# A fused attention and FP4 network block on one core: projection lead, network lag and the place of a rounding changed

## The chip, the core and the metric

The kernel runs on one core of one Trainium2 chip. The metric is device time in microseconds (us) of one execution, as the median of several runs; lower is better. The core has five engines that work side by side, each through its own written list of instructions: TensorE (PE, matrix products, with PEld for its weight loads), VectorE (DVE), ScalarE (ACT), GpSimd (POOL) and SyncE (SP), which here issues every DMA.

## What is computed

`x` is 8 sequences of 1024 tokens with 512 features, all float32. Cut to what matters:

```python
xn  = layernorm(x)
qkv = xn @ W_attn + b_attn                      # 512 -> 3 x 512, 16 heads of 32
att = softmax(causal(q @ k.T * 32 ** -0.5)) @ v
attn = att @ W_proj + b_proj
# network: weights [1408, 512], [1408, 512], [512, 1408]; fq = blockwise FP4 round trip
g, u = fq(xn) @ fq(w_gate).T, fq(xn) @ fq(w_up).T
net  = fq(silu(g) * u) @ fq(w_down).T
out  = x + attn + net
```

`fq` scales each block of 16 values by its largest magnitude over 6, rounds to the FP4 grid and scales back. It is applied to the weights, to `xn` and to the hidden values.

## The kernel before

The work comes in 64 tiles of 128 tokens (8 per sequence) and 64 units of attention: a unit is two heads of one sequence, so a sequence has 8 units. Loops run over tiles, units and weight pieces; each is a Python generator that issues some instructions and then says how long it thinks they take.

- `prepare` and `project` take two tiles at a time: normalise (L398 to L405), transpose on PE (L351, copied out by ACT at L352), multiply with the attention weights (L466 for q and k, L511 for v). ACT takes q and k from PSUM with bias and scale (L478, into `full`, two buffers) and v (L522, `full` too). The inner function `split` writes the part of `full` that the float32r format holds to `high` (L491) and what is left to `low`, in place of `full` (L492). Both go to DRAM (L497), and v too (L527). The first AHEAD tiles multiply with attention weights that are kept on chip; the others stream theirs through a ring of DMA loads (L235).
- `weights_quantised` takes the network's weights in 34 pieces of 128 rows and up to 512 columns: DMA load (L367), ten DVE instructions of the FP4 round trip (L320 to L344), transposes on PE (L351), a copy by ACT (L352).
- `maxima` of a unit: scores for the row maxima and sums on PE (L597, float32r, with high and low parts stacked), the maxima on DVE (L610, L622), an exp with a running sum on ACT (L568), then small statistics, one transpose (L655), a round trip through DRAM (L663 to L676) that puts the shifts where PE needs them.
- `weigh` of a unit: transposed scores with the shift added by a second product (L724, L727), exp on ACT (L735), the causal triangle on POOL (L741), the product with v on PE (L706), a copy by ACT (L769).
- `network` of a tile: gate and up products (L831), silu on ACT (L843), product on DVE (L848), the FP4 round trip on DVE, transposes on PE (L351, L352), down product (L809).
- `finish` of a tile: fetch the attention output, add and scale (L927, L928), output product (L936), add (L941), store.

All engines' lists are written by a planner that runs when the kernel is built. It keeps a clock of its own and, for ACT, DVE and POOL, the time when each is expected to be free (`act`, `dve`, `pool`, called with guessed durations). `Later` puts an action on a list of due times. A `Stream` is a row of parts, each with a position at which it begins and a length, counted in units; `merge` picks, of the streams that lie least far along and whose inputs are thought ready, the next to issue. PE's six PSUM banks are handed out by `Banks`; PE, ACT, DVE and SP then run the lists in order, each instruction waiting for its data and its buffer.

The order of the whole: first a phase with the first eight tiles' projections beside weight pieces; then q, k and v of the first units are loaded (L540, L552); then a second phase up to AHEAD tiles, with more weight pieces and the maxima of unit 0; then the main merge. There, with positions counted in units: unit n is weighed at n; maxima of unit n at n - 1.3; the network of tile n at n + LAG, preceded by what is left of the weight pieces, spread over the first LAG units; the FP4 input of tile n at n + LAG - 1; the projection of tile pair n at n - AHEAD; the output of tile n at n + LAST. EARLY is the number of weight pieces spread over the two phases before.

Of the kernel before, what the change touches and what calls it, by code (L numbers as in the profile page):

```python
# [27 lines left out]
def kernel(  # L28
# [31 lines left out]
    nc = tc.nc  # L60
# [6 lines left out]
    NT = S // P  # L67
# [5 lines left out]
    assert NU == NT  # L73
    QG = 4
    W = QG * P
    AHEAD = 2 * NT
    LAG = 2
    LAST = NT + 2
    SOONER = 0.3
    QUEUE = 2.0  # L80
# [76 lines left out]
    def dve(us, after=0.0):  # L157
        return on("dve", us, after)
# [294 lines left out]
    def project(batch, xnT, g, after, first):  # L453
        yield 0.0, after, 1
        for s in range(2):
            for f in range(0, NC, 2):
                if first:
                    halves = [w[:, :, :] for w in resident_a[s * NC + f : s * NC + f + 2]]
                else:
                    wa = ring_a.take()  # L460
                    halves = [wa[:, :, j * P : (j + 1) * P] for j in range(2)]
                k, bank = banks.take()
                pq = bank.rearrange("p (j t) -> p j t", j=2)
                for j in range(2):
                    for c in range(NC):
                        nc.tensor.matmul(  # L466
                            pq[:, j, :],
                            lhsT=halves[j][:, c, :],
                            rhs=xnT[:, c, :],
                            start=(c == 0),  # L470
                            stop=(c == NC - 1),
                        )
                if not first:
                    ring_a.load_in(3.44 + HOP)
                settle(stored)
                full = p2.tile([P, 2, QW], F32, name="full")
                for j in range(2):
                    nc.scalar.activation(  # L478
                        full[:, j, :],
                        pq[:, j, :],  # L480
                        AF.Identity,
                        bias=bqk[:, s, f + j : f + j + 1],
                        scale=SCALE if s == 0 else 1.0,
                    )
                    end = act(QW, clock[0] + 1.7 * (j + 1))
                banks.back(k, end)
                high = p2.tile([P, 2, QW], F32R, name="high")
                low = full.bitcast(F32R)

                def split(full=full, high=high, low=low):  # L490
                    nc.vector.tensor_copy(high, full)  # L491
                    nc.vector.tensor_tensor(low, full, high.bitcast(F32), ALU.subtract)  # L492
                    dve(1.15)

                def store(s=s, f=f, high=high, low=low):
                    for piece, part in ((0, high), (1, low)):
                        nc.sync.dma_start(  # L497
                            out=batch.qk[s, piece, f : f + 2, :, g * QW : (g + 1) * QW].rearrange("f p t -> p f t"),
                            in_=part.bitcast(F32),
                        )  # L500

                stored.append(Later(end - clock[0] - 0.3, split))
                stored.append(Later(end - clock[0] + 2.0, store))
                yield 3.44, 0.0, 1
        for f in range(0, NC, 2):
            wa = resident_a[2 * NC + f // 2] if first else ring_a.take()
            k, bank = banks.take()
            pv = bank.rearrange("p (i t) -> p i t", i=QT)
            for i in range(QT):
                for c in range(NC):  # L510
                    nc.tensor.matmul(  # L511
                        pv[:, i, :],
                        lhsT=xnT[:, c, i * P : (i + 1) * P],
                        rhs=wa[:, c, :],
                        start=(c == 0),
                        stop=(c == NC - 1),
                    )
            if not first:
                ring_a.load_in(3.44 + HOP)
            settle(stored)  # L520
            v_out = p2.tile([P, QT, 2 * P], F32, name="full")
            nc.scalar.copy(v_out, pv)  # L522
            end = act(W, clock[0] + 3.44)
            banks.back(k, end)

            def store(f=f, v_out=v_out):
                nc.sync.dma_start(  # L527
                    out=batch.v[g * QT : (g + 1) * QT, :, f * P : (f + 2) * P].rearrange("t p e -> p t e"), in_=v_out
                )

            stored.append(Later(end - clock[0] + 0.5, store))
            yield 3.44, 0.0, 1
# [516 lines left out]

    N = B * NT  # L1050
    PIECES = sum((w.shape[0] // P) * -(-w.shape[1] // CW) for w in (w_gate, w_up, w_down))
    EARLY = PIECES - 6
    tiles = [Tile(n) for n in range(N)]
    units = [Unit(n) for n in range(N)]
    batches = []
# [2 lines left out]
    with tc.manual_schedule(  # L1058
        engines={
            mybir.EngineType.PE,  # L1060
            mybir.EngineType.Activation,
            mybir.EngineType.DVE,
            mybir.EngineType.Pool,
            mybir.EngineType.SP,
        }
    ):
        for tl in tiles[:QT]:
            load_tokens(tl)
        for k in range(2 * NC):
            w = p8.tile([P, NC, P], F32, name="pr")  # L1070
            nc.sync.dma_start(out=w, in_=wa_in[:, :, k * P : (k + 1) * P])
            resident_a.append(w)
        nc.sync.dma_start(out=bqk, in_=b_attn[0 : 2 * D].rearrange("(s c p) -> p s c", p=P, c=NC))
        nc.vector.tensor_scalar_mul(bqk[:, 0, :], bqk[:, 0, :], SCALE)
        passed(3.0)
        for tl in tiles[:QT]:
            normed(tl)

        weights_steps = weights_quantised()
        for col in range(2 * D, 3 * D, 2 * P):  # L1080
            w = p2.tile([P, NC, 2 * P], F32, name="wa")
            nc.sync.dma_start(out=w, in_=wa_in[:, :, col : col + 2 * P])
            resident_a.append(w)
        part, late = EARLY * 0.25, [0.0]

        def prepared(first, last):
            return itertools.chain(*(prepare(n) for n in range(first, last, QT)))

        merge(
            [  # L1090
                Stream([(prepared(0, NT), 10.8 * NT, 0.0, 1.0)]),
                Stream([(up_to(weights_steps, part, late), part, 0.0, 1.0)]),
            ]
        )
        settle(stored)
        ring_p.load()
        for n, h in ((0, 0), (0, 1), (1, 0), (1, 1)):
            load_half(units[n], h)
        load_values(units[0])
        net = network(tiles)  # L1100
        TILE = sum(4 * 1.72 * w / CW + w / P * 0.97 for _, w in chunks)

        def first_maxima():
            yield 0.0, clock[0] + 6.0, 1
            yield from maxima(units[0])

        merge(
            [
                Stream([(prepared(NT, AHEAD), 10.8 * NT, 0.0, 1.0)]),
                Stream([(up_to(weights_steps, part, late), part, 0.0, 1.0)]),  # L1110
                Stream([(first_maxima(), 6.0, 0.3, 0.7)]),
            ]
        )
        ring_a.load()
        ring_a.load()
        load_biases()

        def last_weights():
            for half in range(2):
                wp = p2.tile([P, NC, 2 * P], F32, name="wa")  # L1120
                nc.sync.dma_start(out=wp, in_=wp_in[:, :, half * 2 * P : (half + 1) * 2 * P])
                resident.append(wp)
            yield 0.0, 0.0, 0

        def networks():
            yield weights_steps, (PIECES - EARLY) * 0.5, 0.0, LAG
            for n in range(N):
                yield up_to(net, TILE), TILE, n + LAG, 1.0

        def preparations():  # L1130
            for n in range(AHEAD, N, QT):
                yield prepared(n, n + QT), 10.8 * QT, n - AHEAD, QT
            yield last_weights(), 1.0, N - AHEAD + 1, 0.0

        merge(
            [
                Stream((weigh(un), 17.5, un.n, 1.0) for un in units),
                Stream((maxima(un), 6.0, un.n - 1 - SOONER, 1.0) for un in units[1:]),
                Stream(networks()),
                Stream((quantised(tl), 0.45, tl.n + LAG - 1, 0.5) for tl in tiles),  # L1140
                Stream(preparations()),
                Stream((finish(tl), 4.5, tl.n + LAST, 1.0) for tl in tiles),
            ]
        )
        passed(100.0)
# [37 lines left out]
```

## Time and profile before

| what | value |
|---|---|
| median of 3 runs (lowest, highest) | 4255.48 us (4254.81, 4258.41) |
| profiled execution, its own time | 4251.42 us |
| its span | 4249.7 us |
| mean granted PE clock | 0.991 |
| instructions | 58555 |
| HBM read, written | 400.56 MB, 169.35 MB |
| chain that ended last: PE, ACT, DVE | 82%, 7%, 4% |
| first L597, first L724, first L831 | 174.9, 290.8, 363.8 us |
| last L724 | 4121.8 us |

The span runs from the first to the last instruction of the profiled execution; its own time has 1.7 us more around it. An engine's busy time is the time in which at least one of its instructions was running; matmul records overlap, so the mean duration of a record is longer than the pace at which records follow each other. A float32 matmul of the program leaves two records, a float32r one (L597, L724, L727) one. From 860.9 us (unit 10) to 3160.9 (unit 46) the trace repeats itself every two units, 127.8 us each time.

### The profile page before, as it was taken

The page shows a single profiled execution, that of the slowest core. Times are in us where ns is not written, and L with a number is a line of the kernel's source. Part 1 is how long each engine was busy: PE and PEld are TensorE (multiplying, and loading weights), DVE is VectorE, ACT ScalarE, POOL GpSimd, SP SyncE. Part 2 cuts the span into 40 slices and gives each one's busy share as a digit, 9 for nine tenths or more (in the row PEclk, how much of TensorE's full clock was granted, in tenths as well). Part 3 has the DMA queues.
Part 4 walks back from the last instruction along what each step waited for, and adds up shares of the span by engine and source line. Part 5 has one row for each costly group of instructions (what it writes and reads, how often), then busy time and mean ns, then how long its engine had stood idle before and what let it go on. Part 6 is the DMA issues. An engine that isn't in the chain of part 4 may idle for free.

```text
span 4249.7 us, 58555 instructions
## 1 busy us (share of the span) xinstructions
PE 4131.2 (97%) x17684; PEld 2619.1 (62%) x17684; DVE 2763.2 (65%) x7323; ACT 2321.8 (55%) x5918; POOL 546.5 (13%) x1296
## 2 busy tenths in 40 slices
PE   7789999999999999999999999999999999999998
PEld 6666666666666666666666666666666555555555
DVE  6786765666575666575666575666565666667755
ACT  2246556565555565555565555565555666666640
POOL 0001111111111111111111111111111111111110
PEclk9889999999999999999999999999999999999999
DMA  5654434455455455455455455455454433333314
GB/s 183 177 173 129 124 103 120 118 157 157 132 155 150 140 164 153 132 156 151 140 160 155 134 154 149 141 162 153 138 149 131 117 92 94 95 92 93 93 56 126
DMA packets 564187, 573.84 MB, mean 135 GB/s; under 512 B 114976, under 2 KB 420128, under 8 KB 563872
## 3 DMA queue, kind: packets, MB, share of 16 engines
q1 hardware_dynamic: 563872, 570.10, 48.3%
q8 instruction: 142, 2.33, 0.2%
q14 instruction: 173, 1.42, 0.1%
HBM read 400.56 MB, written 169.35 MB: 134 GB/s over the span
## 4 chain that ended last, share of the span: by engine, by line
PE 82%; ACT 7%; DVE 4%; DMA 1%; issue 1%; SPq 0%; ACTq 0%; POOL 0%; DVEq 0%
PE bank L831 26%; PE acc L809 12%; PE bank L466 8%; PE y L706 7%; PE bank L724 6%; PE bank L727 6%; PE bank L597 5%; PE bank L936 5%; PE bank L511 4%; ACT bank L568 3%; PE bank L351 2%; ACT L568 1%; ACT L843 1%; ACT pr L735 1%; DMA ks<-y_kept 1%
## 5 line engine op out<-in xcount | busy, mean ns | idle before, releaser
L568 ACT ACTIVATE bank<-bank,neg 128x512 f32<-128x512 f32 (+3 forms) x1536 | 856.7, 559 | 163.7 <-DVE neg L610 119.8
L735 ACT ACTIVATE pr<-bank 128x512 f32<-128x512 f32 (+3 forms) x1536 | 662.7, 494 | 482.6 <-PE bank L727 478.2
L741 POOL TENSOR_SCALAR_AFFINE_SELECT pr<-pr 128x128 f32<-128x128 f32 x1024 | 393.2, 397 | 3238.3 <-ACT pr L735 3228.9
L610 DVE CUSTOM_DVE_ANT_0 bank<-bank,mask 128x128 f32<-128x128 f32 (+3 forms) x1024 | 501.2, 500 | 469.5 <-PE bank L597 455.7
L724 PE MATMUL bank<-shT,pick 128*128 128x512 f32 (+3 forms) x1536 | 683.8, 453 | 2.7 <-DVE hid L848 1.5
L831 PE MATMUL bank<-wuT,xqT 128*128 128x512 f32 (+1 forms) x1536 | 676.1, 565 | 3.9 <-ACT bank L568 1.0
L809 PE MATMUL acc<-wdT,hqT 128*128 128x512 f32 x1408 | 665.4, 596 | 1.3 <-ACT hqT L352 1.3
L831 PE MATMUL bank<-wgT,xqT 128*128 128x512 f32 (+1 forms) x1536 | 662.9, 561 | 0.0
L597 PE MATMUL bank<-ks,qs 128*128 128x512 f32 (+3 forms) x1536 | 636.2, 475 | 24.7 <-ACT bank L568 21.7
L727 PE MATMUL bank<-qs,ks 128*128 128x512 f32 (+3 forms) x1536 | 516.9, 346 | 0.0
L622 DVE TENSOR_REDUCE neg<-bank 128x1 f32<-128x512 f32 x512 | 345.7, 685 | 186.8 <-PE bank L597 185.6
L597 PEld LDWEIGHTS bank<-ks,qs 128*128 128x128 f32 x1536 | 277.5, 191 | 234.1 <-issue 111.3
L831 PEld LDWEIGHTS bank<-wuT,xqT 128*128 128x128 f32 x1536 | 277.0, 190 | 228.8 <-issue 158.9
L831 PEld LDWEIGHTS bank<-wgT,xqT 128*128 128x128 f32 x1536 | 280.0, 190 | 219.3 <-issue 151.9
L724 PEld LDWEIGHTS bank<-shT,pick 128*128 128x128 f32 x1536 | 290.4, 189 | 155.7 <-issue 78.9
L809 PEld LDWEIGHTS acc<-wdT,hqT 128*128 128x128 f32 x1408 | 255.3, 190 | 197.0 <-issue 183.6
L478 ACT ACTIVATE full<-bank,bqk 128x256 f32<-128x256 f32 x256 | 107.4, 470 | 491.1 <-PE bank L466 409.3
L727 PEld LDWEIGHTS bank<-qs,ks 128*128 128x128 f32 x1536 | 290.6, 189 | 110.6 <-issue 77.1
L466 PE MATMUL bank<-xnT,wa 128*128 128x256 f32 x1536 | 349.8, 381 | 0.9 <-ACT xnT L352 0.6
L466 PEld LDWEIGHTS bank<-xnT,wa 128*128 128x128 f32 x1536 | 288.4, 190 | 55.6 <-issue 18.9
L706 PE MATMUL y<-pr,vs 128*32 128x512 f32 (+3 forms) x3072 | 316.5, 501 | 0.8 <-POOL pr L741 0.8
L568 ACT ACTIVATION_READ_ACCUMULATOR bank<-bank,neg 128x1 f32 x1536 | 315.4, 205 | 0.0
(99 smaller groups left out, 4674.7 us busy)
## 6 DMA issues: line engine op xcount, KB each, us to landing
wa<-in_L_attn_W_attn_dram SPq DMA_DIRECT2D x146, 512.0 KB
qs<-qk_kept SPq DMA_DIRECT2D x512, 128.0 KB
ks<-qk_kept SPq DMA_DIRECT2D x512, 128.0 KB
wp<-in_L_attn_W_proj_dram SPq DMA_DIRECT2D x81, 512.0 KB
qk_kept<-high SPq DMA_DIRECT2D x128, 256.0 KB
qk_kept<-full SPq DMA_DIRECT2D x128, 256.0 KB
y_kept<-yu SPq DMA_DIRECT2D x256, 128.0 KB
yT<-y_kept SPq DMA_DIRECT2D x112, 256.0 KB
```

Source lines behind the costliest of these rows:

```text
L466: nc.tensor.matmul(pq[:, j, :], lhsT=halves[j][:, c, :], rhs=xnT[:, c, :], start=(c == 0), stop=(c == NC - 1),)
L568: nc.scalar.activation(part, part, AF.Exp, bias=neg[:, kind, k + j : k + j + 1], scale=1.0 if kind == 1 else -1.0, accum_out=sums[:, kind, ...
L597: nc.tensor.matmul(sc[:, j * n : (j + 1) * n], lhsT=un.qs[Q][:, r, i * P : (i + 1) * P], rhs=un.ks[h][:, r, :n], start=True, stop=True,)
L610: nc.vector.tensor_tensor_reduce(part, part, mask[:, W - n :], scale=-1.0, scalar=3e38, op0=ALU.add, op1=ALU.min, accum_out=neg[:, kind, k ...
L622: nc.vector.tensor_reduce(neg[:, kind, k : k + 1], sc[:, :n], AX.X, ALU.max, negate=True)
L706: nc.tensor.matmul(y[row : row + HD, q0:], lhsT=un.vs[h][:, jj, r * HD : (r + 1) * HD], rhs=pr[:, q0:], start=(j < 2), stop=(j >= last - 1 ...
L724: nc.tensor.matmul(w[:, q0:], lhsT=pick[:, Q * HU + r, :], rhs=un.shT[:, q0:], start=True, stop=False)
L727: nc.tensor.matmul(w[:, q0:], lhsT=un.ks[h][:, r, jj * P : (jj + 1) * P], rhs=un.qs[Q][:, r, q0:], start=False, stop=True,)
L735: nc.scalar.activation(pr[:, q0:], w[:, q0:], AF.Exp)
L741: nc.gpsimd.affine_select(out=pr[:, q0 : q0 + P], in_=pr[:, q0 : q0 + P], compare_op=ALU.is_ge, fill=0.0, base=0, pattern=[[1, P]], channe ...
L809: nc.tensor.matmul(tl.acc, lhsT=job.hqT[:, j, :], rhs=wdT[:, i, :], start=(i == 0), stop=(i == NI - 1))
L831: nc.tensor.matmul(job.g, lhsT=job.tl.xqT[:, c, :], rhs=wT[:, c, job.i0 : job.i0 + job.w], start=(c == 0), stop=(c == NC - 1),)
```

## The change

Three constants of the plan and one instruction are changed, with what depends on them.

```diff
-    AHEAD = 2 * NT
-    LAG = 2
+    AHEAD = 12
+    LAG = 5
...
                 def split(full=full, high=high, low=low):
-                    nc.vector.tensor_copy(high, full)
+                    nc.scalar.copy(high, full)
+                    rounded = act(W)
                     nc.vector.tensor_tensor(low, full, high.bitcast(F32), ALU.subtract)
-                    dve(1.15)
+                    dve(0.7, rounded + 0.1)
...
-    EARLY = PIECES - 6
+    EARLY = PIECES - 22
...
-        part, late = EARLY * 0.25, [0.0]
+        part, late = EARLY * 0.5 / AHEAD, [0.0]
...
-                Stream([(up_to(weights_steps, part, late), part, 0.0, 1.0)]),
+                Stream([(up_to(weights_steps, part * NT, late), part * NT, 0.0, 1.0)]),
...
-                Stream([(prepared(NT, AHEAD), 10.8 * NT, 0.0, 1.0)]),
-                Stream([(up_to(weights_steps, part, late), part, 0.0, 1.0)]),
+                Stream([(prepared(NT, AHEAD), 10.8 * (AHEAD - NT), 0.0, 1.0)]),
+                Stream([(up_to(weights_steps, part * (AHEAD - NT), late), part * (AHEAD - NT), 0.0, 1.0)]),
```

NT is 8 and PIECES 34. So 12 tiles instead of 16 are projected before the main merge, with 12 planned weight pieces instead of 28; the projections of the main merge begin with tile 12 at position 0; the network of tile n stands at n + 5 instead of n + 2, and the other 22 pieces are spread over five units instead of six over two. The copy that rounds q and k to their high parts is issued on ACT, and the planner is told so. The planner's clock moves with these numbers, so the interleaving of all five lists changes from the second pair of tiles on. Lines after 491 stand one lower in the changed kernel.

## Prediction

> **What bounds the kernel now.** I read the page first: busy time, then the slices.
>
> ```profile
> PE 4131.2 (97%) x17684; PEld 2619.1 (62%) x17684; DVE 2763.2 (65%) x7323; ACT 2321.8 (55%) x5918; POOL 546.5 (13%) x1296
> PE   7789999999999999999999999999999999999998
> PEclk9889999999999999999999999999999999999999
> ```
>
> PE is busy almost all the time, and its dips lie in the first three slices (106 us each) and the last. Only those ends can give much. So I cut the span into stages, at marks of the trace: 15.5 first matmul, 120.5 eight tiles projected, 174.9 first L597 (maxima of unit 0), 272.7 its L655, 290.8 first L724 (unit 0 begins), 332.7 and 381.9 first L724 of units 1 and 2; then a pair of units in the middle, a pair after the last projection, and after the last unit the networks and the last outputs. Columns: stretch, length, busy time of PE, PEld, DVE, ACT, POOL (instructions), granted clock, DMA share, GB/s.
>
> ```profile
> 15.50:120.50 105.00, 97.72 (x457) 84.83 (x458) 82.45 (x186) 25.86 (x56) 5.74 (x9) 0.97 0.50 162
> 120.50:174.90 54.40, 29.14 (x142) 25.37 (x140) 30.69 (x71) 9.38 (x19) 1.14 (x2) 0.78 0.74 192
> 174.90:272.70 97.80, 78.79 (x373) 67.11 (x371) 89.46 (x218) 37.24 (x98) 3.67 (x6) 0.90 0.53 170
> 272.70:290.80 18.10, 14.04 (x53) 11.21 (x54) 7.09 (x27) 3.77 (x13) 0.00 (x0) 0.67 0.33 105
> 290.80:332.70 41.90, 40.06 (x200) 27.05 (x199) 40.32 (x110) 28.86 (x84) 7.04 (x20) 1.00 0.70 201
> 332.70:381.90 49.20, 44.75 (x189) 26.22 (x188) 31.05 (x97) 39.83 (x114) 6.50 (x20) 0.90 0.43 115
> 2010.90:2138.70 127.80, 127.32 (x550) 80.75 (x549) 81.13 (x218) 72.09 (x186) 17.12 (x40) 1.00 0.54 149
> 3395.10:3502.20 107.10, 105.59 (x447) 62.17 (x445) 74.85 (x202) 67.46 (x174) 15.87 (x38) 1.00 0.37 92
> 4127.10:4208.60 81.50, 74.67 (x221) 38.43 (x220) 44.05 (x91) 9.99 (x17) 2.53 (x2) 1.00 0.26 79
> 4208.60:4249.70 41.10, 31.11 (x129) 24.85 (x127) 16.17 (x31) 0.00 (x0) 0.00 (x0) 0.96 0.76 215
> ```
>
> Every engine's instructions stand in a written order, so each stage can be counted. I give each instruction its mean duration from the costliest groups, and a matmul the pace at which it follows its like (0.43 us for a 512-column F32 record, 0.22 for 256 columns). Result: 174.9 to 272.7 has 97.9 us of DVE work, unit 0 41.9 of DVE, unit 1 49.0 of ACT: exactly their lengths. There PE waits for DVE or ACT. A middle pair has 120.4 us of PE work in 127.8; of the 7.4 over, most goes with the L706 blocks (entering one costs 0.45, leaving it 0.2) and 1.2 is L597 waiting for L568.
>
> **The change, part by part.**
>
> ```profile
> L492 DVE TENSOR_TENSOR full<-full,high 128x512 fp32r<-128x512 f32 x128 | 89.3, 697 | 4.4
> L491 DVE CAST high<-full 128x512 fp32r<-128x512 f32 x128 | 54.8, 428 | 147.0 <-ACT full L478 147.0
> L522 ACT COPY full<-bank 128x512 f32<-128x512 f32 x64 | 37.5, 586 | 157.3 <-PE bank L511 88.8 <-issue 39.2 <-DMA qk_kept<-full 24.7
> ```
>
> *Rounding.* DVE loses 128 casts of 428 ns (54.8 us), ACT gains 128 copies. No ACT copy from SBUF is in the trace; bounds are the cast, 0.43, and twice L522, 1.17; I take L522's 0.586, same shape: 75 us. Behind PE both are covered: ACT rises from 72 to 74.4 us of 127.8 per pair. What queues behind the copy on ACT are the exps that free PE's banks; uncovered in every pair it costs 4 x 0.586 = 2.3 us, 49 over 21 pairs. The written order puts L597's run of four just behind a heavier ACT stretch than before, like the pairs after the last projection, where the excess is 8.3, not 7.4. I take +0.5 per pair, bounds -1.2 (all of that L597 wait goes) and +2.3.
>
> *Twelve tiles, twelve pieces.* Ahead of unit 0 stood 16 tiles and 31 started weight pieces; now 12 and 15. A piece is ten DVE instructions, 5.0 us by their groups. The first eight tiles hold 89.7 us of PE and 78.8 of DVE (before 90.6 and 96.0 in 105): 15.5 + 89.7 + 12 of gaps = 117 (gaps were 14.4). Then 15.5 of projection to the first L597, some 1 us of gaps (133.5), and up to L655 33.4 of PE, 39.8 of DVE, 33.0 of ACT where DVE had 97.9. One old stall stays in place: 35 DMA issues (wp, q, k, v; 137.7 to 157.3 in the timeline) hold SP for 20 us, and behind them the q and k stores that give ACT its two `full` buffers back; I give it 10 us. 133.5 + 39.8 + 10 = 183. L655 to unit 0 is written as before: 18 us. Unit 0 begins at 201, bounds 190 (no stall) and 212 (stall twice).
>
> ```profile
> PE bank L351 <- DVE hid L344: 28.7, 3, 12.8
> ACT full L522 <- DMA qk_kept<-full: 24.7, 7, 5.1
> ```
>
> The first of these waits, PE for a weight piece before 290 us, goes; the second stays.
>
> *Network five units behind.* Units 0 to 4 now run without a network, with the other pieces beside them. Units 0 to 3: maxima 4 x 17.6, 19 pieces x 5.0, five tiles' norms and splits x 2.95 = 180.4 us of DVE (48.1, 42.0, 45.1, 45.1), 157 of ACT, 118 of PE. Unit 4 has 43 L597 instead of 24: 57.5 of ACT. Unit 5 is PE's again: 40.2 x 1.06 = 42.6. By the rule that units 0 and 1 show, 180.3 + 57.5 + 42.6 = 280 us. The sums overstate a little, since instructions overlap: over the whole span DVE's is 3106 and its busy time 2763.2, 0.89 of it. So the floor is units 0 to 4 at DVE's 227.8 x 0.89 with 96% busy, its best (unit 0): 211, and 42.6 for unit 5: 254. The ceiling is the 78% busy of units 0 and 1 together: 227.8 x 0.89 / 0.78 + 42.6 = 303. I take 280, by the unit rows, which are nearest.
>
> [...] The row first: in 120.50:174.90 PE was busy 29 of 54 us and its clock was 0.78. [...] By the row units 0 to 4 need 156 us of PE / 0.78 = 200, still under 238 of DVE and ACT, and nothing is added. [...]
>
> *Middle and end.* Units 6 to 9 have 226.9 of PE: + 2 x 7.4 + 4 for two ACT-heavy stretches in unit 8 = 246. Units 10 to 51 are 21 pairs of 127.8 + 0.5 = 2694 (four units more with projections). Units 52 to 61: 5 x 107.1 = 535. Unit 62: 48.3 + 3.1 = 51. Unit 63's attention: 39.6 + 2.7 = 42. Networks alone hold 172 us of PE instead of 73.3; those 73.3 took 81.5, 3.4 of it the last drain: 172 x (1 + 4.8 / 73.3) + 3.4 = 187. Last outputs: 5 tiles alone instead of 8, 27.5 instead of 41.1.
>
> *DMA.* Four tiles more stream their weights (12 wa loads), and the output weights stay resident from unit 53, not 49 (8 wp loads): 20 x 512 KB on SP. DMA is half busy; each issue is about 0.43 us of SP, 9 us in all, beside PE. Uncovered, 10.5 MB at 215 GB/s would be 49. Table loads fall from 188 to 180, 10 us of ACT, covered.
>
> **Sum:** 201 + 280 + 246 + 2694 + 535 + 51 + 42 + 187 + 27.5 = 4264 us of span, against 4249.7: +14. The profiled execution took 4251.42 (1.7 outside the span), a little under the three runs; I add 14 to their median: 4269. About 0.33% slower, where 0.2% (8.5 us) is what a measurement can tell from no change.
>
> In words: unit 0 begins 90 us sooner, but 43 us of projection and 7 of weight transposes move behind it, three networks (91) move behind unit 63, and the units without a network run at DVE's pace with PE half idle.
>
> **Rivals.**
> *The pieces fill DVE across unit borders (faster).* If units 0 to 5 run at their floor of 254, the sum is 4238 of span, 4244; with unchanged pairs too, 4234. For it: unit 0 ran with DVE 96% busy, and pieces are work that waits for no one. Against: units 0 and 1 together took 91.1 for 71.4 of DVE and 68.7 of ACT, 78%. It decides below about 258 for the six units (-8.5 net of the +14).
> *Nothing to tell.* Six units at 270 and pairs unchanged: 4264 - 10 - 10 = 4244 of span, 4250; anywhere from 4247 to 4264 counts.
> *ACT's copies show in the middle (slower still).* +2.3 per pair instead of +0.5: 4264 + 38, 4307. Against: ACT is 58% busy there, and nobody waited for L491 in any pair.
> *It doesn't do what it says.* Excluded for the order (200 program matmuls of q and k stand before unit 0 instead of 264, the first L831 in unit 4, not 1); open only for the copy's price.
>
> **How the numbers follow.** Slower as summed 0.42, ACT showing 0.10, nothing to tell 0.18, faster 0.30. Range: down to 4222 (unit 0 at 190, the six units at 254, pairs unchanged: 4269 - 11 - 26 - 10) and up to 4306 (the ACT case; the ceiling of 303 alone gives 4292). The forecast's own range is 4264 to 4292. Slower 0.52, same 0.18, faster 0.30.
>
> **What would show it.** First L724 near 201 (190 to 212); L351's wait for L344 before it gone; the first L724 of unit 6 near 481, DVE over 90% busy in units 0 to 3, PE clock below 1 there; a middle pair at 127.8 to 128.8; 256 us from unit 63 to the end, was 161.4. Wrong if unit 6 begins before 455, if a pair moves by more than 1 us, or if waits of L597 for L568, 23 us now, double.

## The result, and the profile after

The changed kernel takes 4305.12 us (median of 4 runs, 4303.95 to 4308.27) against 4255.45 us (4 runs, 4254.81 to 4258.41) of the kernel before: ratio 1.0117, 95% interval 1.0099 to 1.0134, or 49.7 us slower. The forecast was 4269, slower, with a range up to 4306: direction right, time 36 us short, beyond the forecast's own range (4264 to 4292) and just inside the whole one. The profiled execution took 4304.34 us, span 4302.6, which is 52.9 more than the span before.

The page of the changed kernel: busy time, then the slices for PE and its granted clock.

```profile
PE 4187.1 (97%) x17684; PEld 2621.5 (61%) x17684; DVE 2722.6 (63%) x7195; ACT 2369.1 (55%) x6038; POOL 549.4 (13%) x1296
PE   8799999999999999999999999999999999999999
PEclk9899999999999999999999999999999999999999
```

PE has as many matmuls as before and is busy 56 us longer for them. The last slice, an 8 before, is now a 9. The damage is not in empty slices: it has to be looked for between the marks. The same stages as before, in the changed kernel (columns: stretch, length, busy time of PE, PEld, DVE, ACT, POOL with instructions, granted clock, DMA share, GB/s): eight tiles; to the first L598; to its L656; to unit 0; units 0 to 3; 4; 5; 6 to 9; a middle pair; a late pair; unit 63's attention with the networks and outputs up to 4275; the end.

```profile
15.70:111.90 96.20, 93.51 (x447) 81.44 (x448) 66.77 (x151) 34.95 (x71) 6.95 (x9) 1.00 0.56 183
111.90:128.60 16.70, 15.87 (x82) 13.86 (x81) 4.77 (x9) 4.96 (x10) 0.00 (x0) 1.00 0.85 209
128.60:187.40 58.80, 38.34 (x171) 31.15 (x169) 34.31 (x97) 27.02 (x76) 2.93 (x4) 0.87 0.65 195
187.40:206.30 18.90, 13.66 (x53) 10.79 (x54) 7.08 (x26) 3.80 (x13) 0.00 (x0) 0.77 0.32 100
206.30:382.80 176.50, 161.77 (x781) 107.33 (x779) 153.47 (x426) 124.14 (x354) 31.14 (x76) 0.98 0.62 172
382.80:443.30 60.50, 53.65 (x212) 30.17 (x211) 43.70 (x124) 47.91 (x137) 7.17 (x20) 0.92 0.56 152
443.30:486.50 43.20, 43.20 (x200) 27.03 (x198) 20.56 (x59) 22.63 (x54) 7.94 (x19) 1.00 0.44 115
486.50:739.70 253.20, 248.52 (x1032) 150.99 (x1032) 151.84 (x411) 147.30 (x374) 31.27 (x80) 0.98 0.41 112
2165.60:2294.90 129.30, 128.25 (x550) 80.70 (x549) 80.41 (x215) 73.80 (x188) 17.34 (x40) 1.00 0.53 148
3567.70:3676.00 108.30, 106.54 (x443) 62.35 (x442) 73.47 (x200) 65.90 (x168) 15.93 (x38) 0.98 0.36 89
4095.30:4275.00 179.70, 170.56 (x513) 89.97 (x510) 111.99 (x243) 20.86 (x36) 6.33 (x5) 0.99 0.27 78
4275.00:4302.60 27.60, 23.34 (x94) 16.87 (x92) 9.99 (x19) 0.48 (x1) 0.00 (x0) 0.99 0.46 133
```

Busy time hides slow stretches of PE (its records stretch when their ends wait: in the timeline below five L598 take 2.45 us), so I cut the loss in another way: every matmul of a stretch at its undisturbed pace (0.43 us for a 512-column F32 record, and so on), and the length of the stretch less that sum. Both kernels hold 3869 us of such work.

| stretch | lost before, us | lost after, us |
|---|---|---|
| start to unit 0 | 93.0 | 58.4 |
| units 0 to 5 | 42.7 | 83.7 |
| units 6 to 9 | 17.3 | 26.4 |
| units 10 to 47 | 140.4 | 176.3 |
| units 48 to 62 | 62.7 | 68.3 |
| unit 63 to the end | 24.4 | 20.3 |

So 15.5 of the 52.9 us are lost by unit 10, 41.5 from unit 10 to 62, and 4.1 come back at the end. The middle is dear because a pair of units takes 129.3 us, about every third pair 130.8, where it took 127.8. The rounding's two lines in the groups (busy, mean ns, idle before):

```profile
L493 DVE TENSOR_TENSOR full<-full,high 128x512 fp32r<-128x512 f32 x128 | 90.2, 705 | 317.8 <-ACT high L491 314.0 <-DMA wa<-in_L_attn_W_attn_dram 3.8
L491 ACT CAST high<-full 128x512 fp32r<-128x512 f32 x128 | 81.0, 633 | 0.5
```

And the waits between the eighth tile and unit 0 (total, times, longest):

```profile
ACT full L478 <- DMA qk_kept<-full: 20.6, 2, 18.8
DVE stats L398 <- DMA xt<-in_L_attn_x_dram: 18.2, 1, 18.2
PE bank L598 <- ACT full L478: 12.4, 2, 9.9
```

Where a pair loses is seen in the timeline of PE in the changed kernel, some 30 us into a pair (start, length, line, records; idle before and its releaser in brackets):

```profile
1804.67 0.40 PE L728 MATMUL bank<-qs,ks 128*128 128x512 f32 x1
1805.48 2.45 PE L598 MATMUL bank<-ks,qs 128*128 128x384 f32 x5 [0.41 <-ACT xqT L352]
1808.11 0.49 PE L598 MATMUL bank<-ks,qs 128*128 128x512 f32 x1 [0.17 <-ACT bank L569]
1808.67 1.98 PE L832 MATMUL bank<-wuT,xqT 128*128 128x512 f32 x4
```

Six L598 are written one behind the other. From the start of L728 to that of L832 pass 4.0 us, for some 1.4 us of products at their pace: 2.6 us are lost. The ACT list of the same moment says why:

```profile
1803.85 0.58 ACT L770 COPY yu<-y 128x512 f32<-128x512 f32 x1
1804.32 0.63 ACT L491 CAST high<-full 128x512 fp32r<-128x512 f32 x1
1804.84 0.59 ACT L352 COPY xqT<-bank 128x512 f32<-128x512 f32 x1
1805.31 2.08 ACT L736 ACTIVATE pr<-bank 128x512 f32<-128x512 f32 x4
1807.23 0.71 ACT L569 ACTIVATE bank<-bank,neg 128x512 f32<-128x512 f32 x1
```

Each L598 needs a PSUM bank, and banks come back only when ACT has done L352, then four L736, then the L569. The copy L491 stands in that queue. The kernel before has its longest stall of this kind at a run of four L597, at a cost of 1.2 us a pair. The length of a run alone is not its price. PE in the kernel before, the run of six and the run of four of a middle pair, and the last but one row of the run of four of a late pair:

```profile
2012.25 1.34 PE L597 MATMUL bank<-ks,qs 128*128 128x512 f32 x6
2094.63 1.65 PE L597 MATMUL bank<-ks,qs 128*128 128x512 f32 x3
2096.45 0.50 PE L597 MATMUL bank<-ks,qs 128*128 128x512 f32 x1 [0.17 <-ACT bank L568]
3573.63 0.97 PE L597 MATMUL bank<-ks,qs 128*128 128x512 f32 x2 [1.08 <-ACT bank L568]
```

The run of six takes 1.34 us, its pace, and loses some 0.2; the four of the late pair lose 2.3: from the start of the L351 in front of them (3571.71) to that of the L831 behind them (3575.35) pass 3.6 us, for some 1.4 of products. The changed kernel has a second run of six in each pair, as cheap:

```profile
1847.38 1.34 PE L598 MATMUL bank<-ks,qs 128*128 128x512 f32 x6
```

By the lists, what differs is what ACT has to do first: in the kernel before, it has done four L568 between 2009.61 and 2012.07, ahead of the cheap run, and two table loads of 1.28 us and two L843 between 2091.36 and 2094.93, in front of the dear one. In about every third pair the place of the dear run costs 1.5 us more, in another way. One such pair:

```profile
1674.77 2.45 PE L598 MATMUL bank<-ks,qs 128*128 128x384 f32 x5 [0.42 <-ACT xqT L352]
1677.40 0.73 PE L598 MATMUL bank<-ks,qs 128*128 128x512 f32 x1 [0.17 <-ACT bank L569]
1677.96 3.43 PE L832 MATMUL bank<-wuT,xqT 128*128 128x512 f32 x4
```

The waits are the same, but the four L832 behind them take 3.43 us instead of 1.98. Two windows of the changed kernel, the run of L598 and what follows it, show the granted clock (next to last but two):

```profile
1674.00:1677.00 3.00, 2.48 (x7) 0.93 (x5) 2.73 (x7) 3.00 (x7) 0.00 (x0) 1.00 1.02 363
1677.00:1681.00 4.00, 3.83 (x6) 1.71 (x6) 2.06 (x6) 4.00 (x14) 0.00 (x0) 0.57 1.05 255
```

The clock is 1.00 during the run and 0.57 behind it (0.50 in the two us from 1678 to 1680).

### The profile page after: what moved, and what is told of

The parts are those of the page before. It is cut to its first block, busy times and chain, and to the rows that moved or that the text cites. A ratio compares the mean times of both kernels' runs of the same rounds, so it can differ in the third digit from the quotient of the medians.

```text
span 4302.6 us, 58498 instructions
## 1 busy us (share of the span) xinstructions
PE 4187.1 (97%) x17684; PEld 2621.5 (61%) x17684; DVE 2722.6 (63%) x7195; ACT 2369.1 (55%) x6038; POOL 549.4 (13%) x1296
## 3 DMA queue, kind: packets, MB, share of 16 engines
q1 hardware_dynamic: 574432, 580.59, 49.1%
HBM read 411.05 MB, written 169.35 MB: 135 GB/s over the span
## 4 chain that ended last, share of the span: by engine, by line
PE 74%; ACT 6%; DMA 4%; DVE 2%; issue 1%; SPq 1%; ACTq 0%; DVEq 0%
PE bank L832 25%; PE acc L810 12%; PE bank L466 6%; PE y L707 6%; PE bank L725 5%; PE bank L937 5%; PE bank L728 5%; PE bank L598 4%; PE bank L512 4%; PE bank L351 2%; ACT bank L569 2%; ACT pr L736 2%; DMA qs<-qk_kept 1%; DMA yT<-y_kept 1%; DMA xt<-in_L_attn_x_dram 1%
## 5 line engine op out<-in xcount | busy, mean ns | idle before, releaser
L736 ACT ACTIVATE pr<-bank 128x512 f32<-128x512 f32 (+3 forms) x1536 | 659.6, 497 | 543.2 <-PE bank L728 540.8
L569 ACT ACTIVATE bank<-bank,neg 128x512 f32<-128x512 f32 (+3 forms) x1536 | 860.0, 566 | 141.2 <-DVE neg L611 123.4
L598 PE MATMUL bank<-ks,qs 128*128 128x512 f32 (+3 forms) x1536 | 644.7, 475 | 44.1 <-ACT bank L569 19.3
L832 PE MATMUL bank<-wuT,xqT 128*128 128x512 f32 (+1 forms) x1536 | 685.0, 572 | 1.9 <-ACT bank L569 0.6
L725 PE MATMUL bank<-shT,pick 128*128 128x512 f32 (+3 forms) x1536 | 654.4, 435 | 5.1 <-ACT bank L569 2.7
L832 PE MATMUL bank<-wgT,xqT 128*128 128x512 f32 (+1 forms) x1536 | 656.2, 561 | 2.9 <-DVE res L942 0.2
L728 PE MATMUL bank<-qs,ks 128*128 128x512 f32 (+3 forms) x1536 | 512.9, 346 | 0.0
L598 PEld LDWEIGHTS bank<-ks,qs 128*128 128x128 f32 x1536 | 279.2, 191 | 272.1 <-issue 106.2
L832 PEld LDWEIGHTS bank<-wuT,xqT 128*128 128x128 f32 x1536 | 283.9, 193 | 217.9 <-issue 146.9
L832 PEld LDWEIGHTS bank<-wgT,xqT 128*128 128x128 f32 x1536 | 280.1, 190 | 223.2 <-issue 143.3
L466 PE MATMUL bank<-xnT,wa 128*128 128x256 f32 x1664 | 380.8, 382 | 1.7 <-ACT bank L569 0.9
L478 ACT ACTIVATE full<-bank,bqk 128x256 f32<-128x256 f32 x256 | 107.3, 470 | 464.2 <-PE bank L466 414.5
L466 PEld LDWEIGHTS bank<-xnT,wa 128*128 128x128 f32 x1664 | 316.0, 192 | 70.0 <-issue 16.6
L728 PEld LDWEIGHTS bank<-qs,ks 128*128 128x128 f32 x1536 | 290.1, 189 | 90.5 <-issue 59.8
L569 ACT ACTIVATION_READ_ACCUMULATOR bank<-bank,neg 128x1 f32 x1536 | 325.3, 212 | 0.0
```

Source lines behind the costliest of these rows:

```text
L466: nc.tensor.matmul(pq[:, j, :], lhsT=halves[j][:, c, :], rhs=xnT[:, c, :], start=(c == 0), stop=(c == NC - 1),)
L569: nc.scalar.activation(part, part, AF.Exp, bias=neg[:, kind, k + j : k + j + 1], scale=1.0 if kind == 1 else -1.0, accum_out=sums[:, kind, ...
L598: nc.tensor.matmul(sc[:, j * n : (j + 1) * n], lhsT=un.qs[Q][:, r, i * P : (i + 1) * P], rhs=un.ks[h][:, r, :n], start=True, stop=True,)
L725: nc.tensor.matmul(w[:, q0:], lhsT=pick[:, Q * HU + r, :], rhs=un.shT[:, q0:], start=True, stop=False)
L728: nc.tensor.matmul(w[:, q0:], lhsT=un.ks[h][:, r, jj * P : (jj + 1) * P], rhs=un.qs[Q][:, r, q0:], start=False, stop=True,)
L736: nc.scalar.activation(pr[:, q0:], w[:, q0:], AF.Exp)
```

## The experiments

Kernels built on the changed one have its line numbers (L598, L656), those built on the kernel before the old ones (L597, L655). All were timed beside the kernel before; ratios are to it. A pair is two units of the middle.

### Which part of the change makes the loss

**The copy back on DVE, the plan kept** (e1_cast_dve). The changed kernel with one instruction put back; its planner still counts the copy on ACT, so the order stays.

```diff
-                    nc.scalar.copy(high, full)
+                    nc.vector.tensor_copy(high, full)
```

> The changed kernel with its rounding copy given back to DVE and nothing else touched: all lists but DVE's and ACT's stay as they are. Changed kernel: 4305, middle pairs of units 129.3, every third 130.8. Theory A (the copy itself, 0.63 us on ACT in front of the exps that free banks, makes the added wait at the run of six L598 and, where PE then waits long enough, one slow clock stretch): middle pairs fall to 128.3 or less and the third-pair surplus of 1.45 goes, 21 pairs x 1.0 to 1.5 = 20 to 32 us, 4273 to 4285. Theory B (the place of the six L598 in the new order makes it): pairs stay within 0.4, 4297 or more. Before unit 6 both expect within 5 us of the changed kernel's 486.5.

4292.78 us, ratio 1.0085 (1.007 to 1.01): 12.3 us less than the changed kernel, between the ranges of the two theories. Pairs are 128.8 and the dearer third pair is rare. The same run of L598, in its timeline:

```profile
1929.47 2.45 PE L598 MATMUL bank<-ks,qs 128*128 128x384 f32 x5
1932.10 0.50 PE L598 MATMUL bank<-ks,qs 128*128 128x512 f32 x1 [0.17 <-ACT bank L569]
1932.66 1.99 PE L832 MATMUL bank<-wuT,xqT 128*128 128x512 f32 x4
```

The idle 0.41 in front is gone, the slow five behind it is not. So the copy costs 12 us, and +1.0 per pair stays that is not the copy's. That the slow clock needs a wait that is long enough, as theory A has it, was an estimate of mine and is not shown: in the changed kernel the idle stretches are 0.41 and 0.17 us where the clock behind them is 1.00 (1809 to 1811 us), and 0.42 and 0.17 where it is 0.57.

**The copy on ACT in the old order** (e2_cast_act). The kernel before with one instruction changed, nothing told to the planner.

```diff
-                    nc.vector.tensor_copy(high, full)
+                    nc.scalar.copy(high, full)
```

> The kernel before with the rounding copy on ACT and nothing else touched; PE's order is the old one. Theory A (the copy costs wherever it stands): pairs rise from 127.8 by 0.5 to 1.5 while projections run, 10 to 35 us, 4265 to 4290. Theory B (only its place in the new order hurts): within 5 us of 4255. A third reading, that the copy relieves DVE at the start: the stage up to the first L724 shortens by at most 16 casts... 32 x 0.43 = 14 us, 4241.

4253.94 us, ratio 0.9993 (0.9983 to 1.0002): nothing. Pairs 127.8 as before, though the copy is as long here as there:

```profile
L492 DVE TENSOR_TENSOR full<-full,high 128x512 fp32r<-128x512 f32 x128 | 88.4, 690 | 238.6 <-ACT high L491 238.6
L491 ACT CAST high<-full 128x512 fp32r<-128x512 f32 x128 | 80.6, 629 | 0.6
```

Unit 0 begins 3.7 us sooner, which the total does not keep. So the copy costs time in one written order and none in the other. That it is dear where it stands in front of a run that wants its banks is read from the ACT list above.

**Lag 2 in the changed kernel** (e3_lag2).

```diff
-    LAG = 5
+    LAG = 2
```

> The changed kernel with the lag back at 2 (12 tiles first, 12 pieces early, 22 pieces over two units, ACT copy). Theory S (the start is a matter of DVE work that has to be done somewhere: what leaves the start comes back in the units without a network): first L724 at 206, units 0 and 1 at their DVE sums of 81.5 and about 70, unit 63 to the end back at 161, total within 20 us of the changed kernel, 4285 to 4325 if the middle pairs stay at 129.3 to 130. Rival (five units without a network are the loss): 4255 or less.

4362.54 us, ratio 1.0251 (1.0235 to 1.0266), 57 more than the changed kernel and above what I expected. Twenty-two weight pieces now stand in two units, which take 169.6 us with PE busy 112.6:

```profile
206.80:376.40 169.60, 112.58 (x477) 74.25 (x475) 147.22 (x374) 88.81 (x238) 15.88 (x40) 0.80 0.43 122
```

And its order is another again, with pairs of 130.3 and 132.0. About half of the miss is there: units 10 to 51 take 2749 us against 2721 in the changed kernel, and I had not expected that a new lag of 2 brings a third order, dearer than both. Another 18 us lie in units 0 and 1, for which I had added up 151.5.

**Lag 5 in the kernel before** (e4_lag5_before).

```diff
-    LAG = 2
+    LAG = 5
```

> The kernel before with the lag at 5 alone (16 tiles and 28 pieces early, DVE copy). Theory S: units 0 to 4 hold attention, projections and few pieces, 25 to 41 us each by their slowest engine, unit 5 starts the networks, unit 63 to the end is 249 to 256 as in the changed kernel; total within 15 us of before, 4245 to 4270. Rival (five units without a network are the loss, whatever the pieces do): 4290 or more.

4307.06 us, ratio 1.0122 (1.0107 to 1.0137): one constant gives the whole loss of the change. The theory's range is missed; the time is the rival's, but for another reason than the rival's, since 34 us are lost between units 10 and 62, where the networks run. Unit 10 comes only 69.7 us sooner, though three networks (91 us) have left its front, so some 21 are lost there; pairs are 129.1 (shown), some of them 130.8; the end gives about 3 back. The dear run of a pair has five L597 here and loses 2.1 us with the copy on DVE, about what the run of six loses in e1_cast_dve (2.0).

```profile
2086.70:2215.80 129.10, 128.19 (x549) 80.70 (x548) 82.91 (x218) 72.20 (x184) 16.75 (x40) 1.00 0.53 148
```

**The early start alone** (e6_start_only). Twelve tiles and twelve early pieces with lag 2 and the copy on DVE; in the middle its order is that of the kernel before.

```diff
-    AHEAD = 2 * NT
+    AHEAD = 12
...
-    EARLY = PIECES - 6
+    EARLY = PIECES - 22
```

(with the parts of EARLY per phase as in the change)

> The kernel before with the start alone changed: 12 tiles and 12 pieces early, 22 pieces over two units, lag 2, copy on DVE as in the old plan. From unit 3 on its written order is that of the kernel before, so the pairs should be 127.8 by theory C. First L724 at 208; units 0 and 1 at their DVE sums, 91 and 60 (151), then as before with four projections more (46): 4257 - 83 + 60 + 6 + 46 = 4286, 4275 to 4297. Rival (12 tiles at the start shift the pairs whatever the order): over 4310.

4287.77 us, ratio 1.0083 (1.0066 to 1.01), as expected. Unit 0 begins 83 us sooner, unit 10 only 9: units 0 and 1 take 151.7 us, paced by DVE.

```profile
207.40:359.10 151.70, 94.05 (x438) 64.81 (x437) 134.21 (x339) 68.47 (x185) 15.88 (x38) 0.76 0.43 120
```

Pairs are 127.7, and the four projections are paid after unit 47. So the parts do not add: alone the early start costs 33 and lag 5 costs 50, together, with the copy, 50 (36 with the copy on DVE, e1_cast_dve). Lag 5 gives the 22 pieces five units to lie in instead of two; that this is the reason is a reading and was not tested.

**Sixteen tiles, twenty pieces early** (e7_pieces20). The kernel before with eight pieces fewer ahead of unit 0.

```diff
-    EARLY = PIECES - 6
+    EARLY = PIECES - 14
```

> The kernel before with 20 pieces early instead of 28 and nothing else (16 tiles, lag 2, copy on DVE). Theory S (a piece costs what DVE needs, 5 us, wherever DVE decides): start 8 pieces x 5 = 40 us shorter, unit 0 at 252; units 0 and 1 at 70.4 and 51.9 instead of 41.9 and 49.3, 31 us longer; pairs 127.8. Net -5 to -12, 4245 to 4252. Rival (a piece in the first units holds PE up twice, since banks wait as well): 4257 or more.

4257.63 us, ratio 1.0004 (0.9995 to 1.0013): a miss, in the rival's range. Unit 0 begins 35.2 us sooner and units 0 and 1 are as much longer, 126.4 us with DVE at 84%.

```profile
255.50:381.90 126.40, 96.31 (x425) 61.57 (x425) 106.29 (x288) 71.03 (x205) 16.81 (x40) 0.88 0.46 128
```

So a piece costs 4.4 us in either place (35.2 / 8), near its 5.0 of DVE. That banks wait as well, as the rival says, was not told apart from this.

### Whether the middle's loss is the written order

The planner holds the maxima's L597 back until DVE is nearly free, by its own clock, within QUEUE us; the maxima of a unit begin 1 + SOONER units ahead of it. Neither is touched by the change. Moving them changes the order and nothing that is computed.

**QUEUE 1.0 in the changed kernel** (e5_queue1).

```diff
-    QUEUE = 2.0
+    QUEUE = 1.0
```

> The changed kernel with the planner's bound on maxima ahead of DVE, QUEUE, at 1.0 instead of 2.0; nothing else. In its written order no three L598 follow each other in a pair of units; in the changed kernel runs of six and three do. Theory C (a run of six L598 outruns the six banks, which come back at the pace of L569's exps, and that makes the surplus of the middle pairs and their slow clock): pairs of 127.8 or less, no third-pair surplus, 21 pairs x 1.8 = 38 us and the units 6 to 9 some 7 better, 4255 to 4272. Rival (ACT is fuller in every pair, wherever the L598 stand): 129 or more, 4290 to 4310.

4305.27 us, ratio 1.012 (1.0105 to 1.0135): no gain, a miss, and in the rival's range. The runs of six are gone, but the maxima end later, and in half of the pairs the transpose L656 is reached before DVE has the statistics. Timeline of PE there:

```profile
2089.65 1.45 PE L810 MATMUL acc<-wdT,hqT 128*128 128x512 f32 x3
2093.25 0.27 PE L656 MATMUL bank<-ident,stat 128*48 128x128 f32 x1 [2.16 <-DVE stat L652]
2093.70 0.41 PE L598 MATMUL bank<-ks,qs 128*128 128x128 f32 x2 [0.18 <-DMA inv_y<-inv_kept]
2093.95 5.36 PE L466 MATMUL bank<-xnT,wa 128*128 128x256 f32 x16
```

Sixteen L466 take 5.36 us behind the wait; elsewhere they take 3.62 (in the changed kernel, for one). The granted clock was 0.75 from 2093.4 to 2096.8 us. A wait of 2.16 us costs 3.9 here. In the other half of the pairs L656 waits 0.8 us; these take 129.3 as well, and where the rest of their time goes was not followed.

**Pieces 20 and QUEUE 0.5** (e8_pieces20_queue).

```diff
-    QUEUE = 2.0
+    QUEUE = 0.5
```

(on e7_pieces20)

> As the last, with QUEUE at 0.5: no three L597 in a row in the middle pairs, where the kernel before has runs of up to six. Theory C: the 1.2 us that each pair of the kernel before spends on such a run go too, pairs of 126.6 and some 20 us less than the last kernel, 4225 to 4235. Rival (runs of four or so cost nothing that another order does not cost elsewhere): within 6 us of the last kernel.

4348.16 us, ratio 1.022 (1.0205 to 1.0235), 90 more than e7_pieces20 and the widest miss: in the middle, in every second pair L655 waits 4.2 us for the statistics, and such a pair takes 133.3. The others, where it waits 1.2 us, take 126.0.

After these two the theory was: a pair pays for runs of L597 that outrun the banks, and for an L655 that is written too soon, and each can be read from the list. I counted both for several settings and ran three.

**QUEUE 1.0 and SOONER 0.4 in the kernel before** (e9_small_queue_before), **the same in the changed kernel** (e10_small_queue_after), **QUEUE 1.0 and SOONER 0.5 in the kernel before** (e11_half_queue_before).

```diff
-    SOONER = 0.3
-    QUEUE = 2.0
+    SOONER = 0.4
+    QUEUE = 1.0
```

> The kernel before with QUEUE 1.0 instead of 2.0 and SOONER 0.4 instead of 0.3, nothing else. The planner then spreads the L597 more thinly (longest runs of the middle three instead of four to six) and, by a count of the written lists, still leaves 0.4 to 3.2 us between DVE's statistics and the L655 that needs them in units 10 to 47; from unit 48 on this margin is -0.3 to -0.6. Theory (a pair pays for runs of L597 that outrun the banks and for an L655 written too soon, and for nothing else that the planner chooses): the 1.2 us run stall goes, pairs 126.3 to 127.0 instead of 127.8, 18 x 1.1 = 20 less, the last five pairs without projections +1 to +2 each: 4236 to 4246. Rival (what is saved in front of one wait is lost at the next, so a pair stays near 127.8 however the maxima are placed): 4252 to 4262. Third: L655 waits here too and the clock halves behind it, as with QUEUE 1.0 in the changed kernel: above 4275.

> The changed kernel with QUEUE 1.0 and SOONER 0.4. Same counts: longest run of L597 three instead of six, margin at L655 1.4 and 0.1 us instead of below nothing as with QUEUE 1.0 alone. Theory (the changed kernel's middle is dear through its written order, by these two waits): pairs 126.8 to 127.8 instead of 129.6 on average, units 10 to 51 2663 to 2684 instead of 2721, the rest as before: 4248 to 4270. Rival (the two waits are symptoms; ACT's copy and the five-unit lag keep the pair at 129 and more): 4292 to 4310. If the margin of 0.1 is missed, every other unit waits at L655 and half clock follows: 4285 to 4305, and the windows show L655 waiting.

> The kernel before with QUEUE 1.0 and SOONER 0.5: margin at L655 1.9 and 3.4 us in units 10 to 47, longest run of L597 three; from unit 48 on a run of six and margins -0.5 and -1.3. Theory of the two waits: middle pairs 126.0 to 126.8, the pairs from unit 48 on 110 instead of 107.3: 4235 to 4248. Rival (a pair keeps its length however the maxima are placed): 4255 to 4270, since the late pairs lose in any case.

e9_small_queue_before: 4229.12 us, ratio 0.9935 (0.992 to 0.995), 7 better than the theory's range, pairs 125.1 and 127.1 in turn. e10_small_queue_after: 4254.61 us, ratio 1.0003 (0.9994 to 1.0013), within the range: 50.5 us less than the changed kernel, pairs 126.9. e11_half_queue_before: 4204.95 us, ratio 0.9883 (0.9868 to 0.9898), the fastest of all and 30 better than the range, mostly because the late pairs did not get dearer, as assumed, but cheaper (106.3 instead of 107.1). Its pair, with PE busy in all of it:

```profile
2114.90:2240.50 125.60, 125.60 (x551) 80.70 (x549) 81.82 (x218) 72.67 (x184) 15.60 (x40) 1.00 0.55 152
```

All three rivals (a pair keeps its length however the maxima lie) fall. My count of margins does not tell what a late pair costs: in e11_half_queue_before -0.5 and -1.3 did not turn into waits of that size, while in e9_small_queue_before, with -0.3 to -0.6, the first four late pairs took 109.2 to 110.6, more than I had allowed.

**The changed kernel with both waits away, as far as the list shows** (e12_late_queue_after).

```diff
-    QUEUE = 2.0
+    QUEUE = 1.0
...
-                Stream((maxima(un), 6.0, un.n - 1 - SOONER, 1.0) for un in units[1:]),
+                Stream((maxima(un), 6.0, un.n - 1 - (0.6 if un.n < 50 else 0.4), 1.0) for un in units[1:]),
```

> The changed kernel with QUEUE 1.0, SOONER 0.6 for the units up to 49 and 0.4 from 50 on. By the count of the lists L655 has 1.5 and 1.2 us of margin in the middle (1.4 and 0.1 with 0.4 throughout), the longest run of L597 is three, the late units are as with 0.4. Theory (both orders, mended, give the same pair, and what is then left of the change's loss lies in the start and in the units without a network): pairs 125.4 to 126.3 as in the kernel before with QUEUE 1.0 and SOONER 0.5 (125.6) instead of 126.9, 21 x 0.6 to 1.5 less than 4254.6: 4223 to 4242, still 18 to 37 above 4205. Rival (ACT's copy and the lag keep the changed kernel's pair at 126.9 or more in any order): 4250 to 4265.

4250.44 us, ratio 0.9986 (0.9976 to 0.9996). The pair is as the theory said:

```profile
2086.10:2211.90 125.80, 125.69 (x550) 80.34 (x550) 80.87 (x214) 74.70 (x188) 16.41 (x40) 1.00 0.55 152
```

The total is above the theory's range, at the low end of the rival's; the pair decides against the rival, which had 126.9 or more. By the table's measure units 10 to 47 lose 106.0 us here, against 102.3 in e11_half_queue_before, so lag and copy matter little there. But up to unit 10 this kernel loses 190.6 us, the changed kernel 168.5 and e11_half_queue_before 151.8. The waits between 206 and 762 us show what: PE stood 21.2 us for L652's statistics, in the changed kernel 3.4.

```profile
PE bank L656 <- DVE stat L652: 21.2, 10, 4.2
```

In units 0 to 5 DVE has the pieces to do as well, and I read the waits as a setting that fits the middle but is too tight there. Whether a setting of its own for these units gives the 20 us back was not tried.

## Why the prediction was right in direction and 36 us short

| step | predicted | measured |
|---|---|---|
| unit 0 begins | 201 | 206.3 |
| units 0 to 5 | 280 | 280.2 |
| units 6 to 9 | 246 | 253.2 |
| units 10 to 51 | 2694 | 2721.0 |
| units 52 to 61 | 535 | 540.1 |
| unit 62 | 51 | 52.8 |
| unit 63 to the end | 256.5 | 249.1 |

That the time lies inside the stated range is luck. The range's top, 4306, stood for ACT's copies uncovered in every pair, which the runs exclude as the main cause (e4_lag5_before loses as much with the copy on DVE); the forecast's own range ended at 4292.

*Start.* Right in its parts. The wait of L351 for pieces went. The stall behind SP's issues stayed as said: ACT's `full` waited 18.8 us for the store and PE 9.9 for ACT, where I had given 10. The eight tiles ended 5 us sooner than I said; the stretch from the first L598 to L656 was 58.8 us where 49.8 was given, since the norms waited 18.2 us for their DMA at the same time (their first L398 starts at 139.9, ACT's L478 at 141.9).

*Units without a network.* Right in the sum, and nearly so by unit: 49.1, 42.4, 44.6, 40.3, 60.6, 43.1 us against sums of the slowest engine of 48.1, 42.0, 45.1, 45.1, 57.5, 42.6. So the rule read from two units (the engine with the largest sum of mean durations sets the length) held for six more, within 5 us each. The sum is closer than its parts, since unit 3 was 4.8 below and unit 4 3.1 above; and it is a rule of thumb, for ACT was busy only 47.9 of unit 4's 60.5 us. The signs I gave for it held less well: DVE was busy 153.5 of 176.5 us in units 0 to 3, 87% and not over 90%, and the clock was 0.98 there, only just below 1.

*Middle.* This is the term that failed: "+0.5 per pair" was +1.8 (2721.0 / 21 = 129.6). It is 27 of the 39 us by which the span's sum was short, and my own test ("wrong if a pair moves by more than 1 us") says so. The mechanism that I named, L597's run just behind a heavier ACT stretch, was the right one. Its size was not: the late pairs of the kernel before, by which I priced it, lose 0.9 us more than a middle pair (8.3 against 7.4), and I took about half of that. The dear run costs 2.6 us where it cost 1.2, +1.4 in each pair; of this 0.5 is the copy (e1_cast_dve), and the rest comes with the order that lag 5 makes (e4_lag5_before). The sum had no term for the slow clock behind the run (0.57 from 1677 to 1681 us), which adds 1.5 in about every third pair. The test named for it, waits of L597 for L568 that double, did not show it (21.7 us before in the list of waits, where I wrote 23, and 19.3 after): those records stretch instead of waiting, and part of the idle time is put down to L352.

*The copy.* 586 ns was given, 633 measured. The difference between 586 and 633 ns is 6 us of ACT in all; no run tests what it does. The copy's price on the path was 12 us (e1_cast_dve), in the old order none (e2_cast_act).

*The rival "ACT's copies show in the middle"* gave 4307, nearly the measured time, for the wrong reason: lag 5 alone gives 4307 with the copy on DVE. It had +2.3 per pair for four uncovered copies; the copy's part is 0.8. The faster rival fell: units 0 to 5 took 280, not 254, and in e7_pieces20, with fewer pieces to place, DVE was again busy only 84% of the first two units.

*Units 6 to 9* were 7 us longer: unit 6 holds 77.5 us, with five waits of L598 for L569, 1.6 us in all; where the rest goes was not followed. *The end* was 7 us shorter than given: the networks alone run as well as they did before, with 20.3 us lost instead of 24.4.

*DMA.* HBM read 10.5 MB more (411.05 against 400.56), as counted; a wait for these transfers is not among the waits that I found in the middle.

## What to carry to other kernels

Before a shift of work between stages is priced by its engine sums, look at what it does to the written order of the loop that takes most of the time: count the longest run of instructions that each need a buffer of an engine that is behind, and the margin at each instruction that waits for a chain. The length of the run is not enough: a run of six cost 0.2 us where ACT was ahead and 2.6 where it was behind. Here 1.4 us in each of 21 pairs was twice what the start lost. Where one constant moves all five lists, compare best with best: with the maxima set anew for each, the old plan takes 4205 us, the changed one 4250, the best of the few settings tried. So the change still costs 45, but by the table's measure 39 of that up to unit 10 and 4 in units 10 to 47.

## What the runs showed of the hardware

A short wait of PE cost more than its length in some places. In e5_queue1, behind the 2.16 us at L656, 16 L466 took 5.36 us instead of 3.62, 1.74 more, at a granted clock of 0.75 (2093.4 to 2096.8 us); behind three of the ten such waits in units 10 to 47 they took 3.67. In the changed kernel, behind a run of six with idle stretches of 0.42 and 0.17 us and stretched records between them, four L832 took 3.43 instead of 1.98, 1.45 more, at a granted clock of 0.57 (1677 to 1681 us). That was so in about one pair of three; in the pair that is shown first, at 1805 us, the four took 1.98 at a clock of 1.00. What decides between the two was not found. The half clock of which the expectations of e9_small_queue_before and e10_small_queue_after speak was measured in the changed kernel, 0.50 from 1678 to 1680 us; for e5_queue1, to which the first of them refers, the mean of 0.75 is what is shown.

ACT's copy of 128x512 from SBUF took 633 ns in the changed kernel, 586 from PSUM in the kernel before; DVE's cast of the same tile took 428 there.
